# Attention stage: the next batch's normalized rows turned by VectorE blocks and a DRAM copy instead of TensorE, with the products dealt to other steps

## The chip, the cores and the metric

The kernel runs on one core of a Trainium2 chip, in float32. The metric is device time in microseconds, the median of several runs of the whole kernel. The engines are TensorE (PE in the profile; PEld is its weight load), VectorE (DVE), ScalarE (ACT), GpSimd (POOL), and SyncE (SP), whose queue issues nearly all DMAs. Each engine takes its own instructions in order; semaphores tie the engines together.

## What is computed

Four layers follow one another for 8 batches of 512 rows of 512 columns: a grid update, an attention block with an adaptive layer norm and an MLP, an expert MLP, and a low-rank correction. The change touches the attention part alone:

```python
def _ln(x):
    m = jnp.mean(x, axis=-1, keepdims=True)
    v = jnp.var(x, axis=-1, keepdims=True)
    return (x - m) / jnp.sqrt(v + EPS)
...
emb = jax.nn.silu(_sin_emb(timestep)) @ W_ada + b_ada
scale, shift = jnp.split(emb[:, None, :], 2, axis=-1)
x = _ln(src) * (1.0 + scale) + shift
q = (x @ Wq + bq).reshape(B, S, N_HEAD, HEAD_DIM).transpose(0, 2, 1, 3)
k = (x @ Wk + bk).reshape(B, S, N_HEAD, HEAD_DIM).transpose(0, 2, 1, 3)
v = (x @ Wv + bv).reshape(B, S, N_HEAD, HEAD_DIM).transpose(0, 2, 1, 3)
scores = jnp.einsum('bhqd,bhkd->bhqk', q / math.sqrt(HEAD_DIM), k)
scores = scores + attention_bias
scores = jnp.where(src_mask, -jnp.inf, scores.astype(jnp.float32))
probs = jax.nn.softmax(scores, axis=-1).astype(v.dtype)
ctx = jnp.einsum('bhqk,bhkd->bhqd', probs, v)
ctx = ctx.transpose(0, 2, 1, 3).reshape(B, S, D)
x = x + (ctx @ Wo + bo)
```

There are 16 heads of 32 columns. The bias is 8 x 16 x 512 x 512 numbers, 134 MB, and is read once.

## The kernel before

A first stage computes the grid update and the layer norm of batch 0. The attention stage follows, then the MLP and expert stages. The attention stage works on 128 units (b, c, r): batch b, a quad c of four heads, and a row group r (every fourth row, 128 rows). One pass of the main loop, called a step here, deals with one unit, and a batch has the steps t = 4c + r, 0 to 15 (lines 1145 to 1181).

In a step PE turns the softmaxed scores of the unit before (tile tr, line 1053), multiplies every second step by V (ctx, line 1073), and computes the next unit's scores (s, line 1015). Between these, in two halves, it computes one projection for which `fill` (line 931) writes out the step by hand: a q, k or v product of this or the next batch, or an o product of the batch before, 4 k-blocks each. The blocks of scores for quad c are needed at the end of step 4c - 1. DVE adds the bias to the scores and takes the row minimum (line 1030), ACT takes the exponential (line 1035), POOL adds the mask to the bias ahead (line 1006). The biases of a unit (two tiles of 512 KB) are loaded three steps ahead, at the end of a step.

In the background DVE computes the grid update of a later batch (`GRID`, lines 834 to 838, by step), with coefficients that SP loads (line 729): from step 8 of batch b on, batch b + 2 is worked on, until step 8 of the following batch. Its normalized rows lie in `xt[n]`, rows on partitions.

The projections need the rows turned, columns on partitions. `x1_in` (line 597) does that for the batch n = b + 1: 16 TensorE transposes into PSUM (tile xtr), and four evictions that multiply by 1 + scale and add shift, two on DVE (line 610) and two on ACT (line 608). They are called in the middle and after the last k block of batch b, in step 9 (lines 655 to 663). The turned rows lie in two tiles of tag x1, column blocks 0 and 1 in the first, 2 and 3 in the second. In steps 11 to 14 `x1_back` turns them back, row group by row group, and adds the o bias, for the residual.

`inverse` (line 1081) sends the reciprocals of the softmax sums through DRAM (rd, then rbs) at the end of steps 0, 4, 8 and 12; `divide` uses them one step later.

`pin` keeps an instruction in program order on its engine. All loads named above are pinned on SP's queue; the store of a finished batch's rows, `x1d` (line 1175), is not. PSUM tile tag m has one buffer, tr has two. The MLP stage turns rows through DRAM too: DVE transposes 32x32 blocks (line 1445), SP stores 1 MB (td, line 1455) and loads it back in eight pieces of 128 KB (line 1462), and ACT scales the pieces (line 1484).

## Time and profile before

| what | value |
|---|---|
| median of 3 runs | 2684.74 us (2684.26 to 2685.39) |
| the profiled execution, its own time | 2684.17 us |
| its span, first to last instruction | 2682.4 us |
| granted TensorE clock, mean | 0.996 |
| attention stage, first scores to the last batch's end | 71.3 to about 1060 us |
| one batch, batches 1 to 6 | 123.4 to 124.2 us |
| steps 9 of batches 1 to 6 | 11.35 to 12.06 us |
| xtr transposes, of 128x128 | 128 in all, 112 of them for batches 1 to 7 |

A page gives the busy time of each engine with its share of the span and the instructions. A timeline line gives start and length in us, engine, line of the code, operation, tiles written and read, shapes, and a count where several were merged; idle time before it and who ended it stand in brackets. On PE, a float32 product of 128x512 is two instructions. SPq lines are DMA issues of the SP queue, with the time that the issuing took, not the transfer.

### The profile page before, as it was taken

The page shows a single profiled execution, that of the slowest core. Times are in us where ns is not written, and L with a number is a line of the kernel's source. Part 1 is how long each engine was busy: PE and PEld are TensorE (multiplying, and loading weights), DVE is VectorE, ACT ScalarE, POOL GpSimd, SP SyncE. Part 2 cuts the span into 40 slices and gives each one's busy share as a digit, 9 for nine tenths or more (in the row PEclk, how much of TensorE's full clock was granted, in tenths as well). Part 3 has the DMA queues.
Part 4 walks back from the last instruction along what each step waited for, and adds up shares of the span by engine and source line. Part 5 has one row for each costly group of instructions (what it writes and reads, how often), then busy time and mean ns, then how long its engine had stood idle before and what let it go on. Part 6 is the DMA issues. An engine that isn't in the chain of part 4 may idle for free.

```text
span 2682.4 us, 39424 instructions
## 1 busy us (share of the span) xinstructions
PE 2645.3 (99%) x14182; PEld 1959.3 (73%) x14182; DVE 1885.0 (70%) x3444; ACT 1007.6 (38%) x2091; POOL 1479.1 (55%) x1091
## 2 busy tenths in 40 slices
PE   7999999999999999999999999999999999999998
PEld 4455555555555555788888888888888888888887
DVE  7878887888888656576666667656566666666665
ACT  2576767776776766112211211210111211211221
POOL 3455565555565564466465555565545555555543
PEclk9999999999999999999999999999999999999999
DMA  8765756666665554553553454455335445445321
GB/s 313 253 222 195 258 200 226 229 241 232 213 238 200 185 178 150 181 156 98 163 147 93 153 148 132 134 144 166 111 112 199 122 145 196 122 148 194 122 100 42
DMA packets 241760, 460.31 MB, mean 172 GB/s; under 512 B 33848, under 2 KB 77440, under 8 KB 232478
## 3 DMA queue, kind: packets, MB, share of 16 engines
q1 hardware_dynamic: 237754, 447.04, 49.3%
q0 software_dynamic: 3360, 10.68, 3.0%
q8 instruction: 113, 1.85, 0.3%
q14 instruction: 81, 0.66, 0.1%
q10 hardware_dynamic: 452, 0.07, 0.0%
HBM read 398.43 MB, written 55.09 MB: 169 GB/s over the span
## 4 chain that ended last, share of the span: by engine, by line
PE 88%; DVE 5%; DMA 3%; ACT 1%; POOL 1%; issue 1%; SPq 0%; ACTq 0%; POOLq 0%; DVEq 0%
PE u L1218 29%; PE y L1218 29%; PE tr L570 7%; PE s L567 5%; PE ctx L567 4%; PE pv L567 4%; PE pq L567 3%; PE o L567 3%; PE pk L567 3%; DMA gc<-coef_c 1%; DVE x L693 1%; DVE bt L1030 1%; PE l L251 1%; DMA gf<-in_x 1%; POOL bt L1006 1%
## 5 line engine op out<-in xcount | busy, mean ns | idle before, releaser
L1006 POOL TENSOR_TENSOR bt<-bt,mk 128x1024 f32<-128x1024 f32 x256 | 542.1, 2142 | 72.1 <-DMA bt<-in_bias 49.9
L1218 PE MATMUL y<-wo,act 128*128 128x256 f32 x2560 | 566.3, 380 | 0.0
L1218 PEld LDWEIGHTS y<-wo,act 128*128 128x128 f32 x2560 | 484.5, 190 | 71.6 <-issue 6.7
L1035 ACT ACTIVATE bt<-bt,mn 128x512 f32<-128x512 f32 x512 | 365.9, 718 | 78.8 <-DVE mn L1030 77.3
L1030 DVE CUSTOM_DVE_ANT_0 bt<-s,bt 128x512 f32<-128x512 f32 x512 | 331.2, 684 | 4.8 <-PE s L567 4.7
L570 PEld LDWEIGHTS tr<-ident,bt 128*128 128x128 f32 x2048 | 229.0, 141 | 143.8 <-issue 102.3
L1218 PE MATMUL u<-bt,wi 128*128 128x256 f32 x1440 | 330.5, 379 | 0.0
L1224 DVE TENSOR_TENSOR act<-u,u 128x512 f32<-128x512 f32 x256 | 173.2, 684 | 200.9 <-PE u L1218 132.7
L1218 PEld LDWEIGHTS u<-bt,wi 128*128 128x128 f32 x1440 | 273.5, 190 | 37.2
L1062 ACT COPY pt<-tr 128x512 f32<-128x512 f32 x368 | 203.9, 585 | 219.7 <-PE tr L570 214.6
L570 PE MATMUL tr<-ident,bt 128*128 128x128 f32 x2048 | 273.8, 276 | 3.7 <-ACT pt L1062 1.8
L1218 PE MATMUL u<-tb,ws 128*128 128x256 f32 x1024 | 242.2, 379 | 0.0
L1218 PE MATMUL y<-t,s 128*128 128x256 f32 x1024 | 227.8, 380 | 0.0
L1227 POOL TENSOR_TENSOR t<-wo,t 128x512 f32<-128x512 f32 x64 | 106.0, 1678 | 203.8 <-PE y L1218 203.8
L1218 PEld LDWEIGHTS u<-tb,ws 128*128 128x128 f32 x1024 | 194.3, 190 | 26.6 <-DVE tb L1224 0.2
L1218 PEld LDWEIGHTS y<-t,s 128*128 128x128 f32 x1024 | 194.0, 190 | 26.1
L1060 DVE COPY pt<-tr 128x512 f32<-128x512 f32 x144 | 99.4, 691 | 152.4 <-PE tr L570 151.3
L1582 ACT ACTIVATE act<-act,b 128x512 f32<-128x512 f32 x128 | 82.9, 711 | 292.8 <-DVE act L1224 292.8
L1582 ACT ACTIVATE act<-act,bi 128x512 f32<-128x512 f32 x128 | 83.8, 712 | 282.6 <-DVE act L1224 282.6
L1601 ACT COPY u<-u 128x512 f32<-128x512 f32 x64 | 36.4, 569 | 393.2 <-PE u L1218 277.8
L567 PE MATMUL s<-kt,qt 32*128 32x512 f32 x1024 | 178.4, 642 | 1.7 <-DVE mn L1030 1.0
L1224 DVE TENSOR_TENSOR x<-y,x 128x512 f32<-128x512 f32 (+1 forms) x97 | 64.7, 681 | 152.6 <-PE y L1218 102.3
(324 smaller groups left out, 4157.5 us busy)
## 6 DMA issues: line engine op xcount, KB each, us to landing
bt<-in_bias SPq DMA_DIRECT2D x256, 512.0 KB
wo<-in_W SPq DMA_DIRECT2D x32, 1024.0 KB
wi<-in_Wi SPq DMA_DIRECT2D x32, 1024.0 KB
wo<-in_Wo_e SPq DMA_DIRECT2D x32, 1024.0 KB
wi<-in_W SPq DMA_DIRECT2D x28, 1024.0 KB
td<-tt SPq DMA_DIRECT2D x22, 1024.0 KB
bt<-td SPq DMA_DIRECT2D x176, 128.0 KB
gq<-coef_q SPq DMA_DIRECT2D x21, 512.0 KB
```

Source lines behind the costliest of these rows:

```text
L567: pin(nc.tensor.matmul(out, lhsT=lhsT, rhs=rhs, start=start, stop=stop))
L570: pin(nc.tensor.transpose(out, src, ident))
L1006: nc.gpsimd.tensor_tensor(bt, bt, mask[b, r][:, None, :].to_broadcast([P, 2, S]), ALU.add)
L1030: nc.vector.tensor_tensor_reduce(bt[:, i, :], ss[h], bt[:, i, :], -1.0, 3.0e38, ALU.add, ALU.min, mn)
L1035: nc.scalar.activation(bt[:, i, :], bt[:, i, :], AF.Exp, bias=mn, scale=-1.0, accum_out=sums[b, c][:, h, r : r + 1],)
L1060: pin(nc.vector.tensor_copy(pt[:, :, r % 2, :], tr))
L1062: pin(nc.scalar.copy(pt[:, :, r % 2, :], tr))
L1218: pin(nc.tensor.matmul(out, lhsT=lhsT, rhs=rhs, start=start, stop=stop))
L1224: pin(nc.vector.tensor_tensor(out, x, y, op))
L1227: pin(nc.gpsimd.tensor_tensor(out, x, y, op))
L1582: nc.scalar.activation(acts[g][:, k, :], acts[g][:, k, :], func, bias=bi[:, j : j + 1])
L1601: pin(nc.scalar.copy(u1, p[0]))
```

## The change

`x1_in` stays for batch 0. For batches 1 to 7 two functions take its place. `x1_turn(n, h)` handles column blocks 2h and 2h + 1: four DVE transposes of 128x256 (32x32 blocks, written with a stride of four elements) into one tile of tag gc, which both halves use; one store of that tile (512 KB) to a DRAM buffer, one buffer for each half; and eight loads of 64 KB from there into the x1 tile, in pieces of 512 bytes. `x1_scale` then multiplies and adds on ACT, in place, a column block at a time. The first half's turn is called at the end of step 9, the second's in step 10 ahead of the product's first half; the scales of blocks 0 and 1 at the end of step 10, those of 2 and 3 in step 11 ahead of the first half of the next batch's q product.

The products move: q of quads 1 to 3 from steps 0, 4, 8 to 1, 5, 8; k from 1, 5, 9 to 2, 6, 9; o from 2, 3, 6, 7 to 3, 4, 7, 10; v of the next batch from 10, 12, 14, 15 to 12, 14, 15 and step 0 of that batch. q and k of the next batch's quad 0 stay in 11 and 13. The last batch keeps its own list, with the v product added ahead in step 0. `x1_back` moves from steps 11 to 14 to 12 to 15, the store of x1 from step 9 to step 11, the load of coefficient a's first half one step later, and tag ct gets a sixth buffer.

```diff
+        def x1_home(b, c):
+            if c % 2 == 0:
+                x1t[b] = io.tile([P, 2, S], F32, name=f"x1_{b}_{c}", tag="x1", bufs=2)
+            x1s[b, c] = x1t[b][:, c % 2, :]
+            return x1s[b, c], sc1[:, c, b : b + 1], shift[:, c, b : b + 1]
...
+        xtd = [dram.tile([P, 2 * D], F32, name=f"xtd_{h}") for h in range(2)]
+
+        def x1_turn(n, h):
+
+            if h == 0:
+                x1t["turn"] = pp.tile([P, 2, D], F32, name=f"xt_{n}", tag="gc", bufs=3)
+            t = x1t["turn"].rearrange("p a d -> p (a d)")
+            v = t.rearrange("p (m c j r) -> p r c m j", m=4, c=2, r=R)
+            for r in range(R):
+                x = xt[n][:, r, 2 * h * P : (2 * h + 2) * P]
+                pin(nc.vector.transpose(v[:, r], x.rearrange("p (c m j) -> p c m j", c=2, j=RK)))
+            pin(nc.sync.dma_start(xtd[h], t))
+            x1_home(n, 2 * h)
+            x1_home(n, 2 * h + 1)
+            src = xtd[h].rearrange("(o p) (m c x) -> m c p o x", p=RK, m=4, c=2)
+            for c in range(2):
+                for m in range(4):
+                    pin(
+                        nc.sync.dma_start(
+                            x1t[n][m * RK : (m + 1) * RK, c, :].rearrange("p (o x) -> p o x", x=P),
+                            src[m, c],
+                        )
+                    )
+
+        def x1_scale(n, *cs):
+            for c in cs:
+                t = x1s[n, c]
+                pin(
+                    nc.scalar.activation(
+                        t, t, AF.Identity, bias=shift[:, c, n : n + 1], scale=sc1[:, c, n : n + 1]
+                    )
+                )
+
+        def lead(f, g):
+            f()
+            yield from g
...
-                (-2, "q", 0), (-2, "q", 1), (-1, "e", 0), (-1, "c", 0), (1, "g", 0), (2, "a", 0),
+                (-2, "q", 0), (-2, "q", 1), (-1, "e", 0), (-1, "c", 0), (1, "g", 0), (3, "a", 0),
...
+            if b and t == 0:
+                jobs.append(v_block(b, 3))
...
-            elif t in (0, 4, 8):
-                jobs.append(q_block(b, t // 4 + 1))
-            elif t in (1, 5, 9):
-                turn = (lambda c: x1_in(n, c)) if t == 9 else None
-                jobs.append(k_block(b, t // 4 + 1, turn=turn))
-            elif t in (2, 3, 6, 7):
+            elif t in (1, 5, 8):
+                jobs.append(q_block(b, (1, 5, 8).index(t) + 1))
+            elif t in (2, 6, 9):
+                jobs.append(k_block(b, (2, 6, 9).index(t) + 1))
+            elif t in (3, 4, 7, 10):
                 if b:
-                    jobs.append(o_block(b - 1, (2, 3, 6, 7).index(t)))
+                    jobs.append(o_block(b - 1, (3, 4, 7, 10).index(t)))
             elif t == 11:
-                jobs.append(q_block(n, 0))
+                jobs.append(lead(lambda: x1_scale(n, 2, 3), q_block(n, 0)))
             elif t == 13:
                 jobs.append(k_block(n, 0))
-            else:
-                jobs.append(v_block(n, (10, 12, 14, 15).index(t)))
+            elif t:
+                jobs.append(v_block(n, (12, 14, 15).index(t)))
             if n < NB:
-                if t in (11, 12, 13, 14):
-                    jobs.append(x1_back(n, t - 11) for _ in range(1))
+                if t == 9:
+                    jobs.append(x1_turn(n, 0) for _ in range(1))
+                elif t == 10:
+                    jobs.insert(0, lead(lambda: x1_turn(n, 1), jobs.pop(0) if jobs else iter(())))
+                    jobs.append(x1_scale(n, 0, 1) for _ in range(1))
+                if t in (12, 13, 14, 15):
+                    jobs.append(x1_back(n, t - 12) for _ in range(1))
...
-            tag, bufs = (("gq", 2), ("gc", 3))[c // 2] if b == NB - 1 else ("ct", 5)
+            tag, bufs = (("gq", 2), ("gc", 3))[c // 2] if b == NB - 1 else ("ct", 6)
...
-            if now and now[0] and now[1:] == ((2, 1) if now[0] < NB - 1 else (3, 3)):
+            if now and now[0] and now[1:] == ((2, 3) if now[0] < NB - 1 else (3, 3)):
                 nc.sync.dma_start(x1d[now[0] - 1], xt[now[0] - 1])
```

More of the change, by code (lines that the diff above doesn't have):

```diff
@@ L594, in mask_out @@
             mask[b, r] = m
+        def x1_home(b, c):
[3 more added lines that the diff above has]
+            return x1s[b, c], sc1[:, c, b : b + 1], shift[:, c, b : b + 1]
         def x1_in(b, c):
-            tag, bufs = ("tr", 2) if b or c < 2 else (f"s{c}", 1)
+            tag, bufs = ("tr", 2) if c < 2 else (f"s{c}", 1)
             tr = ps.tile([P, R, P], F32, name=f"xtr_{b}_{c}", tag=tag, bufs=bufs)
@@ L601, in x1_in @@
                 tp(tr[:, r, :], xt[b][:, r, c * P : (c + 1) * P])
-            if c % 2 == 0:
-                x1t[b] = io.tile([P, 2, S], F32, name=f"x1_{b}_{c}", tag="x1", bufs=2)
-            t = x1t[b][:, c % 2, :]
+            t, g, h = x1_home(b, c)
             tv, trv = t.rearrange("f (p r) -> f p r", r=R), tr.rearrange("f r p -> f p r")
-            g, h = sc1[:, c, b : b + 1], shift[:, c, b : b + 1]
             if c % 2:
@@ L610, in x1_in @@
                 pin(nc.vector.tensor_scalar(tv, trv, g, h, ALU.mult, ALU.add))
-            x1s[b, c] = t
+        xtd = [dram.tile([P, 2 * D], F32, name=f"xtd_{h}") for h in range(2)]
[30 more added lines that the diff above has]
+            yield from g
         def x1_back(b, r):
@@ L644, in q_block, with k_block @@
             qs[b, c] = t
-        def k_block(b, c, tag="m", turn=None):
+        def k_block(b, c, tag="m"):
             pr = ps.tile([P, S], F32, name=f"pk_{b}_{c}", tag=tag)
-            for k in range(KC):
-                mm(
-                    pr, w["Wk"][:, k, c * P : (c + 1) * P], x1s[b, k], k == 0, k == KC - 1
-                )
-                if k == 1 or k == (2 if turn else 3):
-                    yield
-                if turn and k == 2:
-                    turn(0)
-                    turn(1)
+            half = block(
+                pr, lambda k: w["Wk"][:, k, c * P : (c + 1) * P], lambda k: x1s[b, k]
+            )
+            yield half(0)
+            yield half(1)
             t = pp.tile([P, S], F32, name=f"kt_{b}_{c}", tag="kt")
@@ L660, in k_block @@
             ks[b, c] = t
-            if turn:
-                turn(2)
-                turn(3)
         def v_block(b, m, tag="m", bufs=1):
```

## The prediction

> **What bounds the kernel now.** I read the page first, then the busy times of one whole batch of the attention stage, then TensorE's timeline there. A step is one unit (batch, head quad, row group), and starts where its score products (tile s) start on PE. Batches count from 0, steps of a batch from 0 to 15.

> ```profile
> PE 2645.3 (99%) x14182; PEld 1959.3 (73%) x14182; DVE 1885.0 (70%) x3444; ACT 1007.6 (38%) x2091; POOL 1479.1 (55%) x1091
> ```

> The same columns for batch 4 alone (PE, PEld, DVE, ACT, POOL busy, clock, DMA share, GB/s):

> ```profile
> 581.70:705.30 123.60, 123.32 (x805) 67.29 (x804) 104.02 (x216) 87.76 (x202) 71.77 (x51) 1.00 0.66 225
> ```

> PE has 0.3 us free of 123.6, VectorE (DVE) 19.6: a us taken from PE is a us gained only where DVE, ScalarE (ACT) or a transfer isn't next. TensorE's timeline of steps 9 to 11 of batch 4, which the change rebuilds:

> ```profile
> 647.87 1.85 PE L567 MATMUL s<-kt,qt 32*128 32x512 f32 x8
> ...
> 655.90 1.44 PE L570 MATMUL xtr<-ident,x 128*128 128x128 f32 x8
> 657.18 1.02 PE L567 MATMUL pk<-x,Wk 128*128 128x512 f32 x2
> 658.04 1.39 PE L570 MATMUL xtr<-ident,x 128*128 128x128 f32 x8
> 659.36 1.14 PE L567 MATMUL s<-kt,qt 32*128 32x512 f32 x8
> ...
> 665.77 1.14 PE L567 MATMUL s<-kt,qt 32*128 32x512 f32 x8
> ...
> 672.23 1.88 PE L567 MATMUL pq<-x,Wq 128*128 128x512 f32 x4
> 673.95 0.63 PE L570 MATMUL xb<-ident,x 128*128 128x128 f32 x4
> 674.51 1.14 PE L567 MATMUL s<-kt,qt 32*128 32x512 f32 x8
> ```

> Step 9 lasts 11.49 us, where a plain odd step lasts 8.27 (588.10 to 596.37, step 1): the 16 xtr products cost PE some 2.5 to 3.3 us in each of seven batches. That is the whole prize. At 672.23 stands the point to watch: the second half of the next batch's q product, which needs all four column blocks of the turned rows.

> The change sends these rows through DRAM, so I then read the SyncE queue, which issues the DMAs. First its order in the same steps, then what it waits for in the whole run (us, times, longest):

> ```profile
> 649.09 0.32 SPq L1089 DMA_DIRECT2D rd<-rt  x1
> ...
> 656.42 1.76 SPq L1094 DMA_DIRECT2D rbs<-rd  x4
> 658.35 2.00 SPq L995 DMA_DIRECT2D bt<-in_bias  x4
> 660.40 0.84 SPq L710 DMA_DIRECT2D gg<-coef_g  x1
> ```

> ```profile
> SPq L1462 <- DMA td<-tt: 106.0, 22, 6.7
> SPq L1094 <- DMA rd<-rt: 71.0, 32, 6.8
> ```

> SP stands still from a store's issue to its landing when loads of the same data follow: the 16 KB of rd, issued behind 2 MB of loads, held it from 649.41 to 656.42, and everything behind waited. In steps with an empty DMA queue the same store took 1.43 us from issue to first load (120.01 to 121.44). The MLP stage already turns rows in this way, 1 MB in one store and eight loads:

> ```profile
> 1159.35 0.34 SPq L1455 DMA_DIRECT2D td<-tt  x1
> 1163.23 3.66 SPq L1462 DMA_DIRECT2D bt<-td  x8
> ```

> So 3.88 us for the store alone in the queue, 3.66 us to issue eight loads. Last, what the DMA engines move in these steps (last column), and DVE's transposes (min/median/max, and total with mean):

> ```profile
> 660.00:665.00 5.00, 5.00 (x31) 3.09 (x24) 4.86 (x11) 3.31 (x8) 2.46 (x3) 1.00 0.96 327
> 665.00:670.00 5.00, 5.00 (x51) 2.38 (x51) 4.93 (x14) 2.54 (x7) 1.97 (x1) 1.00 1.05 404
> ```

> ```profile
> L1445 DVE STREAM_TRANSPOSE tt<-h x28: 694/698/703, 1152.9 to 1736.0; 128x512 f32<-128x512 f32 x28
> L1087 DVE STREAM_TRANSPOSE rt<-rs 128x32 f32<-128x32 f32 x32 | 6.8, 211 | 1.1
> ```

> **Removed: 16 transposes and four evictions a batch.** Without them step 9 takes 8.27 + 0.71 (its scores already start 0.71 late, 1.85 against 1.14), so step 10 starts at 647.87 + 8.98 = 656.85 instead of 659.36: 2.5 us earlier. Gone too are DVE's two 0.81 us (L610) and ACT's two 0.78 us (L608).

> **Added on DVE: eight block transposes a batch.** From 211 ns for 32 and 698 for 512 elements, 256 elements cost about 0.44, four of them 1.6 us with their starts overlapped. They write with a stride of 16 bytes, which no DVE row shows. Bounds: 1.6, and twice that, 3.2; below 1.6 is excluded, since the dense row is the same operation. I take 1.6; 3.2 would move the chain below by under 1 us, because SP is later. [...] So the price is the trip.

> **Added: the trip, twice in a row on one queue.** Both halves use one turn tile: DVE's second set overwrites what the first store reads, so it waits for that store. SP takes in order: rbs, biases of step 8, store 0, eight loads, biases of step 9, coefficient g, store 1, eight loads. Worked out for batch 4:
> - DVE ends step 9's softmax at 656.7 and the transposes at 658.3. SP finishes rbs and the first two biases at 659.3 (above), and issues store 0 by 659.7. Ahead lie 1.05 MB of bias, from 659.8 at 327 GB/s until 663.0; store 0 (0.52 MB at 404) until 664.3; 1.1 us to be noticed (1.43 less issue): 665.4.
> - Eight loads: 665.4 + 3.66 = 669.1, landed about 2.2 later, 671.3 (bounds 1.7, from rbs packets, and 3.3, from the MLP's last scale). The ACT scale of blocks 0 and 1 comes behind step 10's exponentials and is no later than q's first half needs.
> - Biases and g: 1.85 us, to 670.95. Store 1 is issued by 671.3. Bias 1.05, g 0.52 and store 0.52 MB from 670.8 at 350 to 404 GB/s end at 676.4; landed 677.5. Loads until 681.2, landed 683.4.
> - Two scales of 0.80 (L825's row), the first products starting after the first: half 1 ends at 685.9. Step 12's scores start there instead of at 674.51: **11.4 us late.** The x1_back of that step moves one step on, and its 0.47 us (step 12's 6.87 less a plain even step's 6.41) with it: 11.9 a batch.

> Behind the waiting scale in ACT's queue stand the copies and exponentials of step 11's second half, behind those PE's transposes of step 12; nothing else can run ahead. Behind the waiting SP stand the biases of steps 9 and 10. Those of step 10 are issued at about 682.2 and land at 686; the mask addition (2 x 2.14 us) ends at 690.3, and step 13's softmax needs it near 693, so that stays covered by 2 to 3 us.

> [...]

> **Moved.** The q, k and o products each go one to three steps later, v's last one to step 0 of its batch: the same 16 blocks for batches 1 to 6, at the same PE price, each still ahead of its first use (q and k of quad c before step 4c). Batch 7 gets one block more, 2 x 1.72 = 3.4 us; batch 0 one fewer, in step 10, inside the new wait, so nothing. o's eviction (0.69 on DVE) goes to steps 3, 4, 7 and 10, the last one among the late steps. The store of x1 and coefficient a go to step 11, out of the filled stretch: I count nothing, since rd waited 6.9 us in batch 0 too, which has no such store. A sixth ct buffer is space alone.

> **Sum.** Batches 0 to 5: 6 x 11.9 = 71.4. Batch 6 has no grid loads (its rd waits 3.3 instead of 7.3): the same chain gives store 0 at 661.6, loads until 665.3, store 1 at 672.3, loads landed at 678.2, half 1 at 680.7: 6.2 + 0.47 = 6.7. Batch 7: 3.4. Together 81.5 us. On the profiled execution of 2684.17 (span 2682.4): 2765.7; the median of the runs is 0.6 above it, so **2766**.

> **Rivals.**
> - *A light queue.* The order stands, but stores meet no backlog: 2.7 us each (between 1.43 for 16 KB and 3.88 for 1 MB). 659.35 → 662.05 → 665.7 → 667.6 → 670.3 → 673.9, landed 675.6, half 1 at 678.1: 4.1 a batch, 7 x 4.1 + 3.4 = 32: **2717**. For it: the x1 store is out of the way. Against: the 1 MB of bias lies just ahead of each store.
> - *The trip is hidden, DVE is next.* From 656.7: transposes 1.6, grid e, ct, w (3.0), half a softmax, transposes, copy, the other half: 666.4 instead of 665.6; then o's eviction and the 4.45 us of grid work put step 11's last softmax at 675.0 against 673.8. What PE gained is gone: +0.3 in six batches, -2.8 in batch 6, +3.4: **2687**. For it: DVE is busy almost without a pause from 658.68 to 671.3 already.
> - *Faster.* The trip is hidden and DVE catches up: steps 9 to 11 at PE's pace last 23.66 instead of 26.67, less 0.47: 2.5 a batch, 7 x 2.5 - 3.4 = 14 us: **2670**. It needs the second half's data by about 668, 11 us after DVE's first transposes begin, where the light queue takes 19.

> **Chances.** Filled queue 0.60, light queue 0.22, DVE next 0.06, faster 0.12. A change of 0.2% (5 us) is about what a measurement of this kernel can tell from none. The range leaves out the last two cases: low 2706, under the light queue; high 2800, the first case with the MLP's slowest loads (5.14 for eight) and landings of 3.3: 4 more a batch, and some more.

> **What would show it.** Right: ACT's scale of blocks 2 and 3 waits for a DMA with some 5 to 10 us before it in each of seven batches, PE has gaps in step 11, SP waits for xtd twice a batch with 5 us or more, steps 9 to 11 last about 38 instead of 26.7. Wrong: no wait at the scale, or SP issuing the loads within 3 us of each store; if DVE's transposes take over 0.9 us each, DVE is the cause instead.

## The result, and the profile after

The changed kernel takes 2772.07 us (median of 4 runs, 2770.38 to 2777.78), the kernel before, run beside it, 2685.06 (4 runs, 2684.26 to 2687.60). The ratio is 1.0326, with a 95% interval of 1.0308 to 1.0344: 3.3% slower. The prediction named 2766. The profiled span is 2768.6 us against 2682.4; the stages behind the attention take what they took, so all 86.2 us lie in it.

First the line of the engines on the page, then batch 4 alone (PE, PEld, DVE, ACT, POOL busy, clock, DMA share, GB/s):

```profile
PE 2676.8 (97%) x14070; PEld 1960.1 (71%) x14070; DVE 1910.0 (69%) x3486; ACT 1016.8 (37%) x2105; POOL 1472.2 (53%) x1091
```

```profile
632.90:767.00 134.10, 127.83 (x786) 67.67 (x785) 106.53 (x221) 88.96 (x203) 71.70 (x51) 0.96 0.65 222
```

TensorE executes 112 products fewer and is nevertheless busy for longer, in a clock of 0.96 instead of 1.00. It stands still for 134.10 - 127.83 = 6.3 us of this batch, where it stood still for 0.3 before. The timeline of TensorE shows where. These are steps 9 to 12 of batch 4, with the idle time of an instruction and its releaser in brackets:

```profile
699.19 1.89 PE L567 MATMUL s<-kt,qt 32*128 32x512 f32 x8
...
708.21 1.14 PE L567 MATMUL s<-kt,qt 32*128 32x512 f32 x8
...
718.27 2.68 PE L567 MATMUL s<-kt,qt 32*128 32x512 f32 x4 [2.53 <-DVE mn L1067]
720.88 3.64 PE L567 MATMUL ctx<-pt,v 128*32 128x256 f32 x32
...
732.26 3.58 PE L567 MATMUL pq<-x,Wq 128*128 128x512 f32 x4 [3.74 <-ACT x L643]
735.77 1.14 PE L567 MATMUL s<-kt,qt 32*128 32x512 f32 x8
```

Step 9 has become 9.02 us long (699.19 to 708.21; the prediction said 8.98), so the 2.5 us of TensorE's turn are indeed gone. Then there are two gaps. The first, in the middle of step 11's scores, ends with a row maximum of VectorE; the second is the point that the prediction watched, the second half of the q product, which ends with ScalarE's scale of the turned rows. From step 9's first score to step 12's it takes 36.6 us instead of 26.6. The queue of SyncE in the same steps:

```profile
707.96 0.95 SPq L1032 DMA_DIRECT2D bt<-in_bias  x2
710.15 0.34 SPq L626 DMA_DIRECT2D xtd<-xt  x1
715.05 3.65 SPq L633 DMA_DIRECT2D x<-xtd  x8
...
720.37 0.38 SPq L626 DMA_DIRECT2D xtd<-xt  x1
720.85 0.60 SPq L1212 DMA_DIRECT2D x1d<-x  x1
727.66 3.64 SPq L633 DMA_DIRECT2D x<-xtd  x8
```

Between the first loads and the second store stand two biases and coefficient g. Both times SyncE issues a store and then stands still until it has landed: 4.9 us from the first store's issue to its first load, 7.3 from the second's. Only after the eight loads of the first half does the second store's turn come. Summed over the run (us, times, longest), by SyncE's waits and then by those of the other engines in the attention stage:

```profile
SPq L633 <- DMA xtd<-xt: 78.1, 14, 7.1
```

```profile
ACT x L643 <- DMA x<-xtd: 38.9, 15, 5.6
...
DVE xt L625 <- DMA xtd<-xt: 11.8, 7, 2.7
```

Every sign that the prediction named is there: two waits a batch for xtd (14 in 7 batches, 5.6 us on average), a scale of block 2 that waits for a load (3.3 to 5.6 us a batch, not 5 to 10), a q product that waits for the scale (40.3 us of weight loads in 14 waits). The last line is the tile shared by both halves: VectorE's second set of transposes waits for the first store.

VectorE's transposes themselves, all 56 of them (min/median/max in ns):

```profile
L625 DVE STREAM_TRANSPOSE xt<-x x56: 594/642/730, 162.8 to 984.1; 128x256 f32<-128x256 f32 x56
```

They cost 0.64 us each, 2.1 for a set of four in batch 4, under the 0.9 that the prediction set as the mark from which VectorE would be the cause.

One thing was not foreseen. Look at the durations behind the gaps: context products of 3.64 us where they took 1.93, a q half of 3.58 where it took 1.88. The busy times by stretch have TensorE's granted clock as the third last number; the stretch behind the first gap:

```profile
718.00:724.00 6.00, 5.73 (x36) 2.24 (x36) 5.83 (x19) 2.98 (x6) 0.98 (x2) 0.54 0.80 243
```

The clock is 0.54 over these six us. Behind the second gap it is 0.57 from 732 to 736, and 1.00 from 736 to 742. Both gaps stand in every batch from 0 to 5: 2.3 to 4.4 us at step 11's scores (3.1 in batch 0, behind a first wait of 1.8), 3.7 to 6.0 at the q half. In batch 6 they are 1.0 and 4.2.

### The profile page after: what moved, and what is told of

Read it like the earlier page. It is cut to its first block, busy times and chain, and to the rows that moved or that the text cites. A ratio compares the mean times of both kernels' runs of the same rounds, so it can differ in the third digit from the quotient of the medians.

```text
span 2768.6 us, 39522 instructions
## 1 busy us (share of the span) xinstructions
PE 2676.8 (97%) x14070; PEld 1960.1 (71%) x14070; DVE 1910.0 (69%) x3486; ACT 1016.8 (37%) x2105; POOL 1472.2 (53%) x1091
## 3 DMA queue, kind: packets, MB, share of 16 engines
q8 instruction: 113, 1.85, 0.3%
## 4 chain that ended last, share of the span: by engine, by line
PE 89%; DMA 4%; DVE 4%; ACT 1%; SPq 1%; issue 1%; POOL 0%; ACTq 0%; DVEq 0%; POOLq 0%
PE u L1255 28%; PE y L1255 28%; PE tr L570 7%; PE s L567 6%; PE ctx L567 4%; PE pq L567 4%; PE pv L567 3%; PE o L567 3%; PE pk L567 3%; DMA xtd<-xt 2%; PE l L251 1%; DVE bt L1067 1%; DVE xt L625 1%; DMA x<-xtd 1%; DVE x L724 1%
## 5 line engine op out<-in xcount | busy, mean ns | idle before, releaser
L570 PEld LDWEIGHTS tr<-ident,bt 128*128 128x128 f32 x2048 | 229.9, 141 | 147.0 <-issue 108.2
L570 PE MATMUL tr<-ident,bt 128*128 128x128 f32 x2048 | 274.6, 277 | 3.4 <-ACT pt L1099 1.8
L567 PE MATMUL s<-kt,qt 32*128 32x512 f32 x1024 | 199.0, 664 | 22.7 <-DVE mn L1067 21.9
L1255 PEld LDWEIGHTS u<-tb,ws 128*128 128x128 f32 x1024 | 194.3, 190 | 26.6 <-DVE tb L1261 0.2
L567 PE MATMUL pq<-x,Wq 128*128 128x512 f32 x256 | 134.9, 655 | 36.6 <-ACT x L643 30.5
```

What stands on the lines that cost most here:

```text
L567: pin(nc.tensor.matmul(out, lhsT=lhsT, rhs=rhs, start=start, stop=stop))
L570: pin(nc.tensor.transpose(out, src, ident))
L1255: pin(nc.tensor.matmul(out, lhsT=lhsT, rhs=rhs, start=start, stop=stop))
```

## The experiments

The theory: the trip through DRAM is a serial chain in SyncE's queue (bias, store, stand still, eight loads, bias, store, stand still, eight loads), which delivers the second half some 12 us after TensorE needs it. Rivals: VectorE's transposes and the tile shared by both halves; the new dealing of the products; a store that takes that long whatever is ahead of it. Lengths of steps below are means over batches 1 to 6. The kernel before took 2684.4 to 2687.3 us beside the different versions, so a difference of 3 us between two versions says nothing.

**The new dealing alone.** The kernel takes the new order of q, k, v and o, and turns the rows with TensorE as before:

```diff
+            if b and t == 0:
+                jobs.append(v_block(b, 3))
-            elif t in (1, 5, 9):
+            elif t in (2, 6, 9):
                 turn = (lambda c: x1_in(n, c)) if t == 9 else None
...
-                jobs.append(v_block(n, (10, 12, 14, 15).index(t)))
+                jobs.append(v_block(n, (12, 14, 15).index(t)))
```

> The new dealing of the products alone; the rows are turned by TensorE in step 9 as before. Theory (the trip through DRAM on one queue is the cost): the dealing moves work of PE without adding any, except one block more in batch 7 (its step 0 took 11.36 us in the changed kernel, 6.41 before) against one fewer in batch 0, so 2685 to 2692 us. Rival (the dealing is the cost): above 2740 us.

Measured: 2692.09 us beside 2686.39, ratio 1.0021 (1.0012 to 1.0031). So the dealing costs 5.7 us of the 87. Most of it is step 0 of batch 7, which grows from 6.41 to 11.36 us with v's last block. The changed kernel shows the same step, v's two halves at 1035.44 and 1038.03 and then

```profile
1041.17 3.70 PE L567 MATMUL pq<-x,Wq 128*128 128x512 f32 x8 [1.25 <-ACT v L706]
```

Two halves of some 1.8 us each, and 1.25 us in which the next product waits for v's eviction out of the same PSUM buffer.

**Without VectorE's transposes.** The stores take the rows as they are, so what comes back is not turned:

```diff
-                pin(nc.vector.transpose(v[:, r], x.rearrange("p (c m j) -> p c m j", c=2, j=RK)))
-            pin(nc.sync.dma_start(xtd[h], t))
+            x = xt[n][:, :, 2 * h * P : (2 * h + 2) * P]
+            pin(nc.sync.dma_start(xtd[h].rearrange("p (r x) -> p r x", r=R), x))
```

> The changed kernel without DVE's eight block transposes: the stores take the normalized rows as they are, so the turned rows are not the right ones, and the second half no longer waits for the turn tile. Theory (trip): store 0 is issued 1 us earlier, the second store stays bound by SP, so the wait at the q product's second half shrinks by 1 to 2 us a batch: 2758 to 2765 us. Rival (DVE's load is the cost: 4.1 us of transposes and 1 to 2 us of waiting for the tile a batch): back to 2690 to 2710 us.

Measured: 2771.75 us, ratio 1.0323 (1.0305 to 1.0340): nothing gained. The gap at step 11's scores has gone, but the q product waits all the longer: in batch 4 its first half 2.4 us, and its second half:

```profile
732.14 3.99 PE L567 MATMUL pq<-x,Wq 128*128 128x512 f32 x4 [9.03 <-ACT x L639]
```

So the first gap stood in front of the second on a chain whose end something else set. The first stores left 0.5 us earlier after step 9's start than in the changed kernel, but their loads came 0.8 us later (means of batches 0 to 5), 6.8 to 7.9 us after the bias ahead of the store was issued. A gain of about 1 us a batch could hide in that, but not 12: VectorE, with its transposes and its wait for the tile, is ruled out as the main cause in the changed kernel.

**The scales and the q product one step later.** q of the next batch moves from step 11 to step 12, its scales with it; k and v follow:

```diff
-            if b and t == 0:
-                jobs.append(v_block(b, 3))
+            if b and t in (0, 1):
+                jobs.append(v_block(b, t + 2))
...
-            elif t == 11:
+            elif t == 12:
                 jobs.append(lead(lambda: x1_scale(n, 2, 3), q_block(n, 0)))
```

> The changed kernel with the scales of blocks 0 and 1 at the end of step 11 and those of 2 and 3, with the q product, in step 12; v products fill steps 14, 15, 0 and 1. Same DVE work, same transfers, one step more for the trip. Theory (trip): the wait at q's second half shrinks from about 3.7 to 2 us or less, and the half clock after it goes in part; 5 to 9 us a batch less: 2705 to 2740 us. Rivals (DVE's load, or DMA bandwidth): within 5 us of the changed kernel, 2767 to 2777 us.

Measured: 2743.87 us, ratio 1.0214 (1.0197 to 1.0231). The q half waits for only 0.6 us (1.1 in batch 0); the gap at step 11's scores stays, and grows to 2.7 to 4.1 us in batches 1 to 5. Step 11 falls from 21.62 to 15.89 us only, and step 3, which now holds k's block just ahead of its first use, rises from 8.92 to 10.36.

**The first half's loads behind the second store.** SyncE issues both stores before any load:

```diff
             pin(nc.sync.dma_start(xtd[h], t))
+            if h:
+                x1_load(n, 0)
+                x1_load(n, 1)
+
+        def x1_load(n, h):
             x1_home(n, 2 * h)
```

> The changed kernel with the first half's eight loads issued after the second store instead of ahead of it, so SP no longer stands waiting for the first store and the second store leaves about 3 us earlier. Same instructions, other order on SP. Theory (two trips in a row on one queue): data of blocks 2 and 3 land about 6 us earlier, the wait at q's second half nearly goes, 4 to 8 us a batch less: 2715 to 2745 us. Rivals (DVE, bandwidth): no change, 2767 to 2777 us.

Measured: 2734.62 us, ratio 1.0175 (1.0158 to 1.0192): 37 us less than the changed kernel. The second store and the loads of batch 4 in SyncE's timeline; the first store stands at 692.42, the last thing ahead of these lines is coefficient g, at 694.04 for 0.90 us:

```profile
700.62 0.34 SPq L626 DMA_DIRECT2D xtd<-xt  x1
701.06 7.88 SPq L638 DMA_DIRECT2D x<-xtd  x16
```

The standing still between store and loads is gone: the sixteen loads follow the second store at once. What SyncE now waits for, from 694.9 to 700.6, is VectorE: its second set of transposes ends at 700.59, and waited for 2.2 us for the first store to let go of the tile. The q half finds its rows; step 11's scores still wait for VectorE's maxima (gaps of 3.7 to 5.2 us in batches 1 to 5).

**The tile alone.** The second half is written over the columns of xt that the first half has already used, so VectorE waits for nothing:

```diff
+            if h:
+                t = xt[n][:, :, 0 : 2 * P]
```

> The changed kernel with the second half's transposes written over the first half's columns of the normalized rows, which nothing reads any more, so DVE does not wait for the first store. Theory (SP's order is the longer chain): the gap at step 11's scores shrinks from 2.5 to 4.4 us to under 2, but the gap at q's second half grows by as much, since SP reaches the second store no earlier: 2765 to 2775 us. Rival (the shared tile is the cause): 20 us and more faster than the changed kernel, below 2750 us.

Measured: 2776.02 us, ratio 1.0324 (1.0307 to 1.0342). As without the transposes: the first gap shrinks to 1.5 us in batch 4 and the second grows to 6.9.

**The stores on ScalarE's queue.**

```diff
-            pin(nc.sync.dma_start(xtd[h], t))
+            pin(nc.scalar.dma_start(xtd[h], t))
```

> The changed kernel with the two stores issued on ScalarE's DMA queue instead of SyncE's; the loads stay. Theory (a store stands behind 1 MB of bias loads in its queue): the store lands in 2.5 to 3.5 us instead of 4.9 to 7, SP waits less, and 2 to 4 us a batch are gained: 2745 to 2760 us. If the queue ahead does not matter: within 5 us of the changed kernel.

Measured: 2741.83 us, ratio 1.0197 (1.0180 to 1.0214), a gain of 30 us and more than expected. The loads of the second half in SyncE's queue in batch 4, then their store in ScalarE's:

```profile
700.99 7.69 SPq L633 DMA_DIRECT2D x<-xtd  x8
```

```profile
697.31 0.35 ACTq L626 DMA_DIRECT2D xtd<-xt  x1
```

The first store, issued at 689.87 beside two biases (689.76), still takes 5.4 us to its first load (695.24), and 5.3 to 8.0 in batches 0 to 5. The second one now leaves at 697.31, ahead of the next biases, because ScalarE's queue doesn't stand behind SyncE's loads. Its first load follows 3.7 us later, when SyncE comes to it, and SyncE waits for the 7 first stores alone (46.4 us). The gain is the order of issue; a queue of its own did not shorten the store that is issued beside a bias (5.3 to 8.0 us, where it was 4.7 to 6.8 in SyncE's).

**One step later, and no shared tile.** The edits of "the scales and the q product one step later" and of "the tile alone" together.

> e4_one_step_later with the second half written over dead columns, as in e10, SP's order as in the change. Theory: e4's gap of 3.6 us at step 11's scores shrinks to about 2, and since the data now come later than q's second half in step 12, some of it comes back there: 2715 to 2735 us.

Measured: 2743.65 us, ratio 1.0208 (1.0191 to 1.0225). No gain over the scales one step later with the shared tile (2743.87), where 10 to 30 us were expected. Step 11 fell from 15.89 to 11.74 us and step 12 rose from 7.73 to 10.77: with VectorE free the second store is still issued only after the first half's loads (in batch 4 store at 701.36, loads from 709.32), and the q half waits again, for 4.1 us there.

**Both later, and no shared tile.** The last version, with all loads behind the second store as well.

> e8 with the first half's loads behind the second store, as in e5. Theory: no wait for the turn tile, data in before q's second half in step 12; what is left is DVE's 4.1 us of transposes ahead of softmaxes in steps 10 and 11, batch 7's extra block (5 us) and k in step 3 (1.4 us a batch): 2700 to 2715 us. If DVE were no bound, 2690.

Measured: 2723.02 us, ratio 1.0142 (1.0122 to 1.0162), 20 us less, and 8 above the expected range. SyncE waits for a store in the whole run for 6.4 us instead of 78.1, and the scales wait for no load. What is left in step 11 (12.19 us) is this, in batch 4:

```profile
684.50 2.68 PE L567 MATMUL s<-kt,qt 32*128 32x512 f32 x4 [1.61 <-DVE mn L1075]
687.11 3.64 PE L567 MATMUL ctx<-pt,v 128*32 128x256 f32 x32
```

VectorE's second set of transposes (681.28 to 683.32) now runs between the two pairs of maxima of step 10, and half of step 11's scores wait for the second pair.

**The second turn at the end of step 10.** The last version once more, with VectorE's second set behind both pairs:

```diff
-                    jobs.insert(0, lead(lambda: x1_turn(n, 1), jobs.pop(0) if jobs else iter(())))
+                    jobs.append(x1_turn(n, 1) for _ in range(1))
```

> The kernel of both late edits without the shared tile (2723.0 us), with one edit more: the second half's four transposes, its store and all loads stand at the end of step 10 instead of between step 10's two pairs of softmaxes. Theory A: what is left of the loss in step 11 (mean 12.2 us, 8.7 before) is VectorE's 2.0 us of transposes ahead of step 10's second pair of softmax maxima, for which TensorE's scores wait (1.6 us in batch 4), and the slow clock behind that gap (scores 2.68 instead of 1.1, context 3.64 instead of 1.9). Then step 11 falls to 8.7 to 9.2 and the time by six times 3.2, to about 2703 us (2698 to 2710); the store leaves some 4 us later and ScalarE's scales still find their rows, or wait for at most 1 us. Theory B: the DRAM trip has no slack: the later store makes the scales of step 12 late, TensorE's second q half waits 2 to 4 us in step 12 and runs at the slow clock behind it; step 12 rises from 7.7 to 11 or more, and the time stays at 2718 to 2730 us.

Measured: 2712.25 us, ratio 1.0101 (1.0084 to 1.0118), the best of the changed versions. Step 11 falls to 9.48 us, near theory A's 8.7 to 9.2. The gap at its scores and the slow clock behind it are gone in batches 1 to 6, and one scale alone waits for a load, for 0.2 us. Step 11's scores and context in batch 4:

```profile
678.79 3.04 PE L567 MATMUL s<-kt,qt 32*128 32x512 f32 x8
681.76 1.93 PE L567 MATMUL ctx<-pt,v 128*32 128x256 f32 x32
```

The median is 2 us outside the expected range, since the second set's 2 us did not disappear. Step 11's eight scores are still spread over 2.5 to 3.0 us in batches 1 to 5, where 1.14 is their pace, and step 12 rises from 7.74 to 8.43, where the q product waits 0.6 to 1.0 us for a scale that stands behind late exponentials. Against the kernel before this version still loses 27.8 us. In its step lengths: 8.3 in steps 0 and 1 of batch 7 (v's two blocks), 6.1 in batch 0, and 2.2 in each of batches 1 to 6. There step 9 wins 2.54 us, and steps 3, 11, 12 and 13 to 15 lose 1.55, 0.70, 1.56 and 0.97. Step 3's loss is k's eviction, for which the first scores of the new quad wait 1.36 us in each of these batches.

**The biases behind the stores.** The changed kernel, with the two bias loads that stood just ahead of each store held until the store is issued:

```diff
             pin(nc.sync.dma_start(xtd[h], t))
+            while held:
+                load_bias(*held.pop(0))
...
+                if now[0] < NB - 1 and now[1:] in ((2, 0), (2, 1)):
+                    held.append(units[i + 3])
```

> The changed kernel (2772 us), with the two 1.05 MB bias loads that SyncE issues just ahead of the two stores held until the store has been issued; everything else in its place. This is the light queue of the prediction's rival. Theory A (a store waits behind the bias that was issued ahead of it): the first loads follow store 0 by about 3.5 us instead of 4.9 to 6.9, the second ones follow store 1 by 3.5 to 4.5 instead of 7.3; both gaps of TensorE shrink, the second one most, and with them the slow clock; 5 to 9 us less a batch, 2715 to 2735 us. Theory B (a store has this latency whatever is ahead of it, and the loads are late because SyncE does everything in turn): stores and loads stay as far apart as they were, 2765 to 2775 us; if the later bias loads reach GpSimd's mask addition late, above 2775 us.

Measured: 2744.47 us, ratio 1.0220 (1.0203 to 1.0237): 28 us less, 9 above the range of theory A. SyncE's waits for the stores fall from 78.1 to 34.5 us. The first loads now follow their store by 3.0 to 3.8 us, but the second ones by 5.4 to 6.7 in batches 0 to 5, not 3.5 to 4.5. In batch 4:

```profile
700.72 0.37 SPq L626 DMA_DIRECT2D xtd<-xt  x1
...
706.52 3.70 SPq L635 DMA_DIRECT2D x<-xtd  x8
```

A bias is issued right behind both stores, so it cannot make the difference between 3.0 to 3.8 and 5.4 to 6.7. Ahead of the second store stands coefficient g, 0.5 MB (700.18), in batches 0 to 5; in batch 6, which has none, the second store takes 3.5 us. So the wait is the traffic that stands ahead of the store, and not a constant: theory B falls.

**Both of the last two.** The second turn at the end of step 10 ("the first kernel" below) and the biases behind the stores, together.

> The first kernel of this call and the second one's edit together: second turn at the end of step 10, scales and q one step later, all loads behind the second store, bias loads behind the stores. If the DRAM trip still limits the first kernel (its theory B), this one gains 10 us or more over it; if not (theory A), the two are within 5 us of each other, near 2700 us, or this one is slower because its bias comes later.

Measured: 2734.03 us, ratio 1.0184 (1.0167 to 1.0201): 22 us more than with the bias ahead, and all of it in step 12 (12.17 us instead of 8.43). The expectation named a bias that comes later. It does: GpSimd waits for it in the attention stage for 118.1 us instead of 63.1. But the loads have lost their slack too. The held biases now stand between the second store and the loads, the first load follows the first store by 10.8 to 10.9 us instead of 8.9 to 9.2 in batches 1 to 5, and the scales wait for loads, where the second turn at the end of step 10 alone had a single wait of 0.2 us:

```profile
ACT x L652 <- DMA x<-xtd: 11.5, 13, 3.9
```

Step 12 is also 2.5 us longer in batch 3, where the scales wait for 0.4 us only; how much each of the two costs no run separates. The mask additions move beside other work of VectorE as well: its product x<-x,gq of 128x1022 at 701.54 takes 3.14 us beside the additions of 701.47, the next one of its kind, at 713.54, 1.21.

**Gaps alone.** The kernel before, with nothing of the change; ScalarE copies one column block of the rows onto itself ahead of the second q half, more often in each batch:

```diff
+        def held_q(n):
+            for _ in range({1: 2, 2: 3, 3: 4, 4: 5, 5: 6, 6: 8, 7: 10}[n]):
+                pin(nc.scalar.copy(x1s[n, 3], x1s[n, 3]))
+            yield from q_block(n, 0)
```

> The kernel before (2684 us), with nothing of the change: in step 11 of each batch ScalarE copies the last column block of the normalized rows onto itself before the second q half that reads it, 2 times in the first batch, then 3, 4, 5, 6, 8 and 10 times, at some 0.7 us each. This makes gaps of TensorE of about 1.0 to 6.6 us in one place, with no turn, no store and no other dealing. Theory A (a gap of TensorE by itself sets its clock back): behind gaps from some 2.5 us on, the four matmuls of the q half take about 3.6 us instead of 1.88, as behind the changed kernel's gaps, and behind the short ones 1.88; the time grows by the gaps, about 24 us, and by 1.7 us for each of the four or five long ones, to some 2715 us. Theory B (the slow clock of the changed kernel comes from the change's traffic or from its load, not from the gap): the four matmuls take 1.88 us behind every gap, and the time is some 2708 us.

Measured: 2712.86 us, ratio 1.0102 (1.0085 to 1.0118). The total lies between the two theories' numbers, and the gaps came out shorter than planned (17.2 us in batches 1 to 6 instead of about 24 in all), so it is the durations behind the gaps that decide. The gap falls inside the half, so two of its four products stand behind it; at full clock two take 1.02 to 1.12 us. They take 1.12 us behind 1.58, 1.57 behind 4.52 and 2.08 behind 5.09 us. The two batches in between:

```profile
554.07 1.32 PE L567 MATMUL pq<-x,Wq 128*128 128x512 f32 x2 [2.50 <-ACT x L632]
...
682.07 1.12 PE L567 MATMUL pq<-x,Wq 128*128 128x512 f32 x2 [2.72 <-ACT x L632]
```

The granted clock tells why. In batches 1 to 6 of this run every slow stretch lasts 3.41 us at a clock of 0.50. The three start at 554.87, 810.86 and 940.57, which is 256.0 and 129.7 us apart, 75 and 38 times 3.41 us. In this run then the slow stretches lie on a grid of 3.41 us. The stretches of that grid around the gaps of 2.50 us (551.57 to 554.07) and 2.72 us (679.35 to 682.07):

```profile
551.46:554.87 3.41, 0.92 (x3) 0.49 (x3) 0.76 (x4) 3.31 (x6) 1.79 (x1) 1.00 0.58 181
554.87:558.28 3.41, 3.41 (x14) 1.27 (x13) 1.82 (x2) 1.61 (x5) 0.04 (x1) 0.50 0.00 1
...
677.75:681.16 3.41, 1.59 (x9) 0.76 (x7) 1.91 (x5) 3.28 (x7) 2.86 (x2) 1.00 0.75 216
681.16:684.57 3.41, 2.50 (x14) 1.25 (x14) 0.80 (x2) 3.30 (x8) 0.00 (x0) 1.00 0.14 53
```

The shorter gap lies whole in one stretch, which leaves TensorE busy for 0.92 us of it, and the next stretch is slow. The longer one is split over two, with 1.59 and 2.50 us busy, and neither is followed by a slow one. In this run, what counts is the idle time within one stretch (2.49 us of it before a slow one, 1.82 before none), and not the length of the gap. So a gap alone sets the clock back, without the change's traffic: theory B falls. But theory A's threshold falls as well. By the steps, the extra cost over the gap itself is 1.6 to 1.8 us in batches 3, 5 and 6 (steps 11 and 12 together, less the steps of before, less the gap) and 0.3 in batches 1, 2 and 4.

## Why the prediction came out right, step by step

**The mechanism.** Store, stand still, loads, twice in one queue: shown. Each edit of the changed kernel that shortens this chain or gives it a step more gains 28 to 37 us (loads behind, stores elsewhere, bias behind; scales later), and neither of the two that only relieve VectorE gains anything. What the prediction drew as one gap came as two, since step 11's scores wait for VectorE, whose second set of transposes stands behind the first store.

**Terms of the sum.** For batch 4, from step 9's first score:
- Step 9: 8.98 predicted, 9.02 measured.
- Transposes: 0.44 each and 1.6 for four predicted, 0.64 and 2.1 measured. The dense rows did not hold for these transposes, which write with a stride of 16 bytes (that the stride is the reason no run separates); inside the bounds of 1.6 and 3.2, and off the chain, as said.
- First store to first load: 5.7 predicted, 4.9 measured (4.7 to 6.8 in batches 0 to 5). Eight loads: 3.66, and 3.65; landed 1.7 us later where 2.2 was taken (731.30 to the scale at 733.02). No run shows the 2.2, which the sum takes for each landing; 1.7 is what was measured in its place.
- Second store to first load: 6.2 predicted, 7.3 measured. The store of x1, 1 MB, which was to be out of this stretch, slips in between the second store and its loads (720.85 above). The prediction counted nothing for it, and rightly: where scales and x1's store came a step later and the tile was not shared, the second store still took 8.0 us to its first load (701.36 to 709.32), with x1's store behind it at 716.82. What is left are the bias and the coefficient ahead of it: priced too low. With the bias held it was 5.4 to 6.7, and without the coefficient too 3.5.
- Last scale to the end of the half: the scale waits 3.3 us (5 to 10 predicted), and the half ends 36.7 us after step 9's start, where 38.0 was predicted. The chain was 1.4 us early in this batch.
- The slow clock, 1.7 us on the q half, was not in the sum. In part it made up for the chain that ended earlier: without it the half could not have ended before the second scale (733.83) and its last two products, some 0.9 us, so it cost 1.1 here. The slow scores and context of step 11 (1.5 and 1.7 us) fall in time that the chain would have left idle.
- A batch: 11.9 us predicted for batches 0 to 5; measured 13.7, 13.5, 11.5, 12.9, 10.5 and 11.4, mean 12.2. Batch 6: 6.7 predicted, 7.8 measured. Batch 7: 3.4 predicted, 5.0 measured, since the eviction of 1.25 us was missed.

The sum was 81.5 us, the spans differ by 86.2: 2 too little for batches 0 to 5, 1.1 for batch 6, 1.6 for batch 7. That it came so close is in part luck. The one batch that was worked out lost 1.4 us less than predicted, batches 0, 1 and 3 lost 1.0 to 1.8 more, and the slow clock, which the sum did not have, stands in every batch.

**The trip beside a step.** Measured in the changed kernel are 4.9 + 3.65 + 1.7 = 10.2 us for batch 4's first trip (1.7 from the last load to the scale that waited for it, read in the second trip), where a plain even step lasts 6.41: one step does not hide it. With the bias held back, a first store takes 3.0 to 3.8 us to its first load instead of 4.7 to 6.8; the rest of the trip is the issuing of eight loads and their landing.

**The rivals.** The light queue was drawn at 2.7 us for a store and 2717 us. With the bias behind the stores it is 3.0 to 6.7 us and 2744: the coefficient was still ahead of the second store. Faster needed the second half within 11 us of the first transposes; in the shortest trips of all versions (both later, no shared tile) the last load is issued 17.4 to 19.1 us after them in batches 0 to 5, and TensorE's saving of 2.54 us a batch is real but lost again elsewhere. DVE next turned up where the trip was out of the way: moving the transposes from between the maxima of step 10 shortened step 11 by 2.7 us, but gained only 10.8 us in all by the medians (7.9 against the kernel before beside each), since part came back in steps 12 to 14.

## What to carry to other kernels

The trip through DRAM cost what stood in the issuing queue between its two ends, above all the standing still between a store and its dependent loads (78.1 us of SyncE's waits here); put all stores ahead of all loads (37 us less here), and ask how much other traffic stands ahead of each store (3.0 to 3.8 us to the first load with the bias held back, 4.7 to 6.8 with it ahead). Where a chain has two gaps in series, removing the first one can show nothing until the last one is gone (2771.75 and 2776.02 us here, beside 2772.07), so test the edits together as well as one by one. As an estimate from the changed kernel, price a stall of TensorE as the gap plus, at worst, work at half clock for 3.4 or 6.8 us: so long the granted clock stood at 0.50 behind the gaps of batches 1 to 6 (10.2 us in batch 0).

## What the runs showed of the hardware that was not expected

A store of 0.5 MB took from 3.0 us (bias held back) to 8.0 us (bias and coefficient ahead of it, 701.36 to 709.32 with the scales one step later and no shared tile) to its first load; on ScalarE's queue a first store beside a bias took 5.3 to 8.0 us, no less than the 4.7 to 6.8 on SyncE's. And of VectorE's 128 x 1022 products in the version with the second turn late and the biases behind the stores, one took 1.21 us and one 3.14, the longer one beside GpSimd's mask additions; that the additions cause it is argued from the two timelines, not shown by a run.
